# Decoder of a four-layer convolution kernel: last step by eight rows, with parts of the next group's front between its halves

## The chip, the cores and the metric

The kernel runs on one core of a Trainium2 chip. The metric is the device time of one execution in microseconds (us). The core has a matrix engine (PE, with its weight loads shown as PEld), a vector engine (DVE), a scalar engine (ACT), a general engine (POOL), and SP, which here only issues transfers (DMAs). Each engine works through its own queue in order, and waits on semaphores where it needs what another engine or a DMA makes. SBUF is the on-chip memory of 128 partitions, PSUM the small memory that PE writes to.

## The reference

Four layers are applied to x, 16 images of 32 channels of 128x128, in float32; each adds its result to its input. The change lies in layer 3, an edge detector followed by a small encoder and decoder. The 16 images of 32 channels are taken as 4 groups of 4 x 32 channels of 128x128.

```python
# layer 3: y = edge operators of x, five of them, concatenated
y = maxpool2(conv3x3(y, conv1_w, conv1_b))      # 128 -> 64
y = maxpool2(conv3x3(y, conv2_w, conv2_b))      # 64 -> 32
y = maxpool2(conv3x3(y, conv3_w, conv3_b))      # 32 -> 16
y = conv3x3(y, conv4_w, conv4_b)                # 16
y = conv3x3(deconv2x2(y, deconv1_w, deconv1_b), conv5_w, conv5_b)   # -> 32
y = conv3x3(deconv2x2(y, deconv2_w, deconv2_b), conv6_w, conv6_b)   # -> 64
y = conv3x3(deconv2x2(y, deconv3_w, deconv3_b), conv7_w, conv7_b)   # -> 128
return x + orig * y                             # orig: x normalised
```

## The kernel before

`network` (line 2137) runs the stages one after another: `layer0`, three stages of layer 1, `layer2`, then `layer3_edges` (line 1436: edge operators, conv1 and its pooling along one axis; result in the DRAM scratch `p1`), and last `layer3_net` (line 1892), everything from conv2 on. This last stage is called the decoder stage here. Its parts:

- **Joint weights** (lines 1903 to 1955). Each deconvolution and the convolution after it are one linear map, so their weights are multiplied once: for k = 5, 6, 7 three loads (`d_t`, `d_b`, `c_t`, each in one buffer), 36 matmuls of 32x32 and nine of one column (each is two passes on PE), a copy to `W`, and eight small DVE operations for a bias and an edge correction (lines 1930 to 1952).
- **front(g)** for one group of four images (all 128 partitions: 4 images x 32 channels). It loads `p1` in eight tiles `pt` of 512 KB (two buffers), takes a maximum on DVE (line 2078) and writes `c2` with two ACT operations each (line 2080). `squares` (line 1980) then gathers shifted copies of `c2` with 16 SBUF-to-SBUF DMAs of 136 KB, so that one matmul sees four pixels x 32 channels as its 128 rows. `conv_pool` (matmuls line 1998) does conv2 and the pooling, 8 PSUM tiles of 16 matmuls; then 16 DMAs of 36 KB, conv3, conv4 (line 354), `windows` (line 2033; 16 DMAs of 36 KB), joint step 5, 16 DMAs of 136 KB, joint step 6 (lines 2046 to 2070). The result is `d3`, one buffer.
- **The last step** of a group: `windows(d3)` makes `w7` with 16 DMAs of 528 KB, all before the first matmul. Then for each q of 8 parts of 16 output rows: load `xs` (1024 KB), normalise it to `xn` on ACT (line 2119), four phases of four matmuls (line 2046), an edge correction per phase (line 2051), a multiply into `xn` (line 2126), the addition of `xs` on DVE (line 2127), and the store of `xn` from ACT's queue (line 2128). `xs` and `xn` have two buffers each.

Each matmul of the decoder has 32 columns of weights and writes 32 partitions; the four images j = 0..3 go to four column tiles of PE, which can work at the same time.

**Order.** Within the decoder stage nothing fixes the order of the engines' queues by hand: the tile framework orders the instructions of each queue by readiness and by their place in the program. Other stages use `in_order` (line 48), which makes the named engines follow the program's order; `layer3_edges` does not. The loop of the stage, before, is

```python
        d3 = front(groups[0])
        for n, g in enumerate(groups):
            w7 = windows(d3, 64, "w7")
            if n + 1 < len(groups):
                d3 = front(groups[n + 1])
            for q in range(8):
                ...
```

so the next group's front stands ahead of this group's eight parts.

**The edge stage's beginning** (lines 1451 to 1527) makes constants in a pool `et`, which is closed before the pools of the strips are opened; the first work on strips is at line 1587, and PE's first work after the constants waits for statistics of two images (line 1648).

Of the kernel before, what the change touches and what calls it, by code (L numbers as in the profile page):

```python
# [10 lines left out]
F32 = mybir.dt.float32  # L11
# [1424 lines left out]
def layer3_edges(tc, w, x3, p1, sb3, b3, groups=range(NG)):  # L1436
# [12 lines left out]
    with ExitStack() as ctx:  # L1449
# [20 lines left out]
        with tc.tile_pool(name="et", bufs=1) as tp:  # L1470
# [56 lines left out]
            V.tensor_scalar_mul(V5[:, 14], V5[:, 14], -1.0)  # L1527
        ap = ctx.enter_context(tc.tile_pool(name="ea", bufs=2))
# [345 lines left out]
        for m, b in enumerate(images):  # L1874
            now = nxt
            more = m + 1 < len(images)
            if more:
                g1, j1 = divmod(images[m + 1], 4)
                t1 = image(g1, j1)
            for n in range(4):  # L1880
                conv(n, now, d)
                if m < 3 or made < 12 * (m + 2) + 4 * n:
                    advance(min(made + 4, 12 * len(images) + 1))
                if n == 2 and more:
                    if m + 1 in cut_at:
                        vec = batch(m + 1)
                    nxt = prepare(g1, j1, t1, *expand(j1), vec)
            if more:
                d = differences(t1)


def layer3_net(tc, w, x3, p1, out, sb3, b3, groups=range(NG)):
# [4 lines left out]
    nc = tc.nc  # L1897
    with ExitStack() as ctx:
        cp = ctx.enter_context(tc.tile_pool(name="fc", bufs=1))
        psum = ctx.enter_context(tc.tile_pool(name="fp", bufs=7, space=PSUM))  # L1900
        psw = ctx.enter_context(tc.tile_pool(name="fpw", bufs=1, space=PSUM))
        wc = {i: load(nc, cp, w[f"c{i}_p"], f"c{i}_p") for i in range(2, 4)}
        wc4 = load(nc, cp, w["c4_w"], "c4_w")
        bb = load(nc, cp, w["l3_b"], "l3_b")

        pairs = {
            (0, 0): [(0, 1)], (0, 1): [(1, 0), (2, 1)],
            (1, 0): [(0, 0), (1, 1)], (1, 1): [(2, 0)],
        }
        joint = {}  # L1910
        with tc.tile_pool(name="fw", bufs=1) as tp:
            for i, k in ((1, 5), (2, 6), (3, 7)):
                wd = load(nc, tp, w[f"d{i}_t"], "d_t")
                bd = load(nc, tp, w[f"d{i}_b"], "d_b")
                wk = load(nc, tp, w[f"c{k}_t"], "c_t")
                pw = psw.tile([P, 4, T], F32, name="pw", tag="pw")
                for s in range(4):
                    first = True
                    for ph in range(4):
                        rows, cls = pairs[ph // 2, s // 2], pairs[ph % 2, s % 2]  # L1920
                        todo = [(dy, dx, p, q) for dy, p in rows for dx, q in cls]
                        for n, (dy, dx, p, q) in enumerate(todo):
                            nc.tensor.matmul(
                                pw[32 * s : 32 * s + 32, ph], wd[:, 2 * p + q],
                                wk[:, 3 * dy + dx, 0:T], start=first, stop=n == len(todo) - 1,
                                tile_position=(0, 32 * s), skip_group_check=True,
                            )
                            first = False
                W = cp.tile([P, 4, T], F32, name=f"W{k}", tag=f"W{k}")
                nc.vector.tensor_copy(W, pw)  # L1930


                pb = psw.tile([P, 4, T], F32, name="pb", tag="pw")
                for t in range(9):
                    nc.tensor.matmul(
                        pb[:, 0, t : t + 1], wk[:, t], bd, start=(t == 0), stop=(t == 8),
                        skip_group_check=True,
                    )
                tb = tp.tile([P, 3, 3], F32, name="tb", tag="tb")
                nc.vector.tensor_copy(tb.rearrange("p a b -> p (a b)"), pb[:, 0, 0:9])  # L1940
                by = tp.tile([P, 2, 3], F32, name="by", tag="by")
                nc.vector.reduce_sum(by[:, 0], tb, AX.X)
                nc.vector.reduce_sum(by[:, 1], tb.rearrange("p a b -> p b a"), AX.X)
                bias = cp.tile([P, 1], F32, name=f"B{k}", tag=f"B{k}")
                nc.vector.reduce_sum(bias, by[:, 0], AX.X)
                nc.vector.tensor_add(bias, bias, bb[:, k - 2 : k - 1])
                edge = cp.tile([P, 8], F32, name=f"E{k}", tag=f"E{k}")
                nc.vector.tensor_scalar_mul(
                    edge[:, 0:4].rearrange("p (a b) -> p a b", b=2), by[:, :, 0:3:2], -1.0
                )  # L1950
                for a in range(2):
                    nc.vector.tensor_copy(
                        edge[:, 4 + 2 * a : 6 + 2 * a], tb[:, 2 * a, 0:3:2]
                    )
                joint[k] = W, bias, edge

# [29 lines left out]
        def conv_pool(i, src, n, put):  # L1986
# [4 lines left out]
            for r in range(0, h, nr):  # L1991
                m = sp.tile([P, nr, h], F32, name="m", tag="m")
                for ph in range(4):
# [11 lines left out]
                    if ph == 0:  # L2005
                        nc.scalar.activation(m, ps, AF.Identity, bias=b)
                    else:
                        nc.vector.scalar_tensor_tensor(m, ps, b, m, ALU.add, ALU.max)
                put(r, m)

# [5 lines left out]
        def pitched(n, tag):  # L2016


            t = bp.tile([P, n + 3, n + 1], F32, name=tag, tag=tag)
# [20 lines left out]
        def phase(k, src, n, ph, i0, nr):  # L2040
# [10 lines left out]
            nc.vector.tensor_scalar_add(ps[:, :, c], ps[:, :, c], edge[:, 2 + b : 3 + b])  # L2051
            if (a == 0 and i0 == 0) or (a == 1 and i0 + nr == n):
                r = a * (nr - 1)
                nc.vector.tensor_scalar_add(ps[:, r], ps[:, r], edge[:, a : a + 1])  # L2054
                o = ps[:, r, c : c + 1]
                nc.vector.tensor_add(o, o, edge[:, 4 + 2 * a + b : 5 + 2 * a + b])  # L2056
            return ps, bias

        def joint_conv(k, src, n, dst):
            nr = min(n, 512 // n)  # L2060
            for i0 in range(0, n, nr):
                for ph in range(4):
# [4 lines left out]
                    if b:  # L2067
                        nc.vector.tensor_scalar_add(o, ps, bias)  # L2068
                    else:
                        nc.scalar.activation(o, ps, AF.Identity, bias=bias)  # L2070

        def front(g):
            c2 = planes(ap, 64, "c2")
            for h in range(4):
                for a in range(2):
                    t = xp.tile([P, 2, 8, 64], F32, name="pt", tag="pt")
                    nc.sync.dma_start(t, p1[g][:, 2 * a : 2 * a + 2, 8 * h : 8 * h + 8])
                    nc.vector.tensor_tensor(t[:, 0], t[:, 0], t[:, 1], ALU.max)
                    for b in range(2):
                        nc.scalar.activation(  # L2080
                            c2[:, a, b, a + 8 * h : a + 8 * h + 8, b : b + 32], t[:, 0, :, b:64:2],
                            AF.Identity, bias=b3[:, g : g + 1],
                        )
            c3 = planes(bp, 32, "c3")

            def put(r, m):
                r //= 2
                nr = m.shape[1] // 2
                for a in range(2):
                    for b in range(2):  # L2090
                        nc.scalar.copy(
                            c3[:, a, b, a + r : a + r + nr, b : b + 16], m[:, a::2, b::2]
                        )

            conv_pool(2, squares(c2, 64, "w6"), 64, put)
            c4 = padded(bp, 16, "c4")
            conv_pool(
                3, squares(c3, 32, "w5"), 32, lambda r, m: nc.scalar.copy(c4[:, 1:17, 1:17], m)
            )
# [3 lines left out]
            nc.scalar.activation(d1[:, 1:17, 1:17], ps, AF.Identity, bias=bb[:, 2:3])  # L2103
            d2 = pitched(32, "d2")
            joint_conv(5, windows(d1, 16, "w5"), 16, d2)
            d3 = pitched(64, "d3")
            joint_conv(6, windows(d2, 32, "w6"), 32, d3)
            return d3

        d3 = front(groups[0])  # L2110
        for n, g in enumerate(groups):
            w7 = windows(d3, 64, "w7")
            if n + 1 < len(groups):
                d3 = front(groups[n + 1])
            for q in range(8):
                xs = xp.tile([P, 2048], F32, name="xs", tag="xs")
                nc.sync.dma_start(xs, x3[g][:, 2048 * q : 2048 * q + 2048])
                xn = xp.tile([P, 2048], F32, name="xn", tag="xn")
                nc.scalar.activation(  # L2119
                    xn, xs, AF.Identity, bias=sb3[:, g, 1:2], scale=sb3[:, g, 0:1]  # L2120
                )
                xv = xn.rearrange("p (i a j b) -> p a b i j", a=2, j=64, b=2)
                for ph in range(4):
                    ps, bias = phase(7, w7, 64, ph, 8 * q, 8)
                    v = xv[:, ph // 2, ph % 2]
                    nc.vector.scalar_tensor_tensor(v, ps, bias, v, ALU.add, ALU.mult)  # L2126
                nc.vector.tensor_add(xn, xn, xs)  # L2127
                nc.scalar.dma_start(
                    out[4 * g : 4 * g + 4].rearrange("b c h w -> (b c) (h w)")[
                        :, 2048 * q : 2048 * q + 2048  # L2130
                    ],
                    xn,
                )
# [252 lines left out]
```

## Time and profile before

| what | us |
|---|---|
| median of three runs | 17326.91 (17290.49 to 17357.52) |
| the profiled execution | 17413.58 |
| its span, first to last instruction | 17411.8 |
| decoder stage in it, from the end of the edge stage's matmuls at 16577 | 835 |
| DVE, POOL and PE busy over the whole span | 14898.3, 9787.4, 15201.4 |
| mean granted PE clock over the span | 0.92 |

All times below are of the profiled execution, in us from the start of its span, so the stage begins at 16577 and ends at 17412. In a view by windows, each row is a stretch of time: its length, busy time (and instruction count) of PE, PEld, DVE, ACT and POOL in it, the granted PE clock, the mean busy share of the 16 DMA engines, and GB/s. In a timeline, a row is a run of equal instructions: start, length, engine, line, operation, output <- input, count, and in brackets the idle time before it with what ended it. "SPq" is SP issuing a DMA. Every matmul of float32 counts as two PE instructions.

### The profile page before, as it was taken

How to read it: one execution, taken by the hardware profiler on the slowest of the kernel's cores; microseconds unless marked ns; L12 is line 12 of the kernel's file. 1: busy time of each engine (PE TensorE's matmuls, PEld its weight loads, DVE VectorE, ACT ScalarE, POOL GpSimd, SP SyncE). 2: the span in 40 equal slices, each digit the busy share in tenths (PEclk: the TensorE clock that was granted, in tenths of full speed). 3: DMA queues.
4: the chain of work that ended last, by engine and by line, in shares of the span. 5: the costliest groups of instructions: out<-in, count | busy, mean ns of one | idle time of the engine just before them, and what ended most of it. 6: DMA issues, size and time to landing. Idle time of an engine off the chain costs nothing. (4 is left out here: it accounts for less than half of the span.)

```text
span 17411.8 us, 300873 instructions
## 1 busy us (share of the span) xinstructions
PE 15201.4 (87%) x113294; PEld 5760.5 (33%) x113294; DVE 14898.3 (86%) x15100; ACT 12226.0 (70%) x23748; POOL 9787.4 (56%) x18465
## 2 busy tenths in 40 slices
PE   8999999999998889888888888899999997688965
PEld 2333333333333322222222222255555553233422
DVE  9999999999999758999899999888888886787623
ACT  7878887878887656777677776588888883465411
POOL 8999999999999617778787787700000000000000
PEclk9999999999999988999899999889999898787888
DMA  0000000000000384444454444477777779544346
GB/s 19 14 12 12 12 12 16 12 12 12 12 12 12 61 149 152 162 160 160 157 166 157 156 161 159 141 198 193 196 204 193 194 194 200 115 82 77 66 134 197
DMA packets 1532120, 1895.18 MB, mean 109 GB/s; under 512 B 150885, under 2 KB 872861, under 8 KB 1519846
## 3 DMA queue, kind: packets, MB, share of 16 engines
q1 hardware_dynamic: 1419558, 1698.68, 37.7%
q10 hardware_dynamic: 84480, 83.91, 1.5%
q0 software_dynamic: 26624, 93.35, 1.5%
q8 instruction: 891, 14.60, 0.3%
q14 instruction: 567, 4.64, 0.1%
HBM read 1560.92 MB, written 229.64 MB: 103 GB/s over the span
## 5 line engine op out<-in xcount | busy, mean ns | idle before, releaser
L235 POOL TENSOR_SCALAR Rp<-su,nv 128x128 f32<-128x128 f32 x16384 | 5807.8, 395 | 142.2 <-PE pS L241 108.5
L224 DVE TENSOR_TENSOR Rd<-pu,nv 128x2048 f32<-128x2048 f32 x2176 | 4878.2, 2277 | 64.3 <-PE pS L241 61.2
L239 ACT ACTIVATE Ra<-su,bv 128x128 f32<-128x128 f32 x14336 | 4284.4, 388 | 601.0 <-PE pS L241 594.3
L241 PE MATMUL pS<-Rd,zw 128*32 128x512 f32 x17408 | 2883.8, 604 | 315.9 <-DVE Rd L224 314.7
L822 DVE TENSOR_TENSOR_SCAN hh<-dd,state,pd 128x512 f32<-128x512 f32 x2304 | 2824.0, 1267 | 165.2 <-PE py L856 23.5
L843 POOL TENSOR_TENSOR hh<-hh,bc 128x2048 f32<-128x2048 f32 x512 | 2318.7, 4529 | 501.3 <-DVE state L830 472.6
L241 PE MATMUL pS<-Rp,zw 128*32 128x512 f32 x8192 | 1937.0, 596 | 145.3 <-POOL Rp L235 140.7
L807 PE MATMUL pd<-du,spread 32*128 32x512 f32 x4608 | 1386.5, 677 | 549.2 <-DVE hh L822 541.0
L1228 POOL DMA_DIRECT2D x<-ob x64 | 90.0, 1407 | 3098.5 <-DVE ob L1227 2762.7
L799 ACT ACTIVATE dd<-dd,m_a 128x512 f32<-128x512 f32 x2304 | 1513.8, 714 | 336.7 <-DMA dd<-dm 324.9
L817 DVE TENSOR_TENSOR pd<-pd,bc 128x1024 f32<-128x1024 f32 x1152 | 1401.4, 1216 | 66.9 <-ACT bc L780 50.6
L1236 ACT ACTIVATE yd<-yd,nrow 128x2048 f32<-128x2048 f32 x512 | 1242.2, 2426 | 41.3 <-DMA yd<-ymap 41.3
L241 PE MATMUL pS<-Ra,zw 128*32 128x512 f32 x7168 | 1256.3, 602 | 0.0
L1116 ACT ACTIVATE ya<-pb,nrow 128x1024 f32<-128x1024 f32 x1024 | 1185.9, 1247 | 83.9 <-PE pb L1115 83.4
L1115 PE MATMUL pb<-Y,sel 32*128 32x512 f32 (+1 forms) x5120 | 1083.5, 741 | 163.4 <-ACT ya L1116 160.2
L241 PEld LDWEIGHTS pS<-Rd,zw 128*32 128x32 f32 x17408 | 603.3, 109 | 1368.1 <-DVE Rd L224 734.0
L807 PEld LDWEIGHTS pd<-du,spread 32*128 32x128 f32 x4608 | 381.6, 195 | 1617.9 <-DVE hh L822 701.1
L1120 DVE TENSOR_SCALAR yd<-yd 128x2048 f32<-128x2048 f32 x512 | 719.9, 1406 | 190.4 <-ACT yd L1236 188.8
L241 PEld LDWEIGHTS pS<-Rp,zw 128*32 128x32 f32 x8192 | 432.4, 110 | 1236.9 <-POOL Rp L235 773.9
L1120 DVE TENSOR_SCALAR ya<-ya 128x2048 f32<-128x2048 f32 x512 | 755.1, 1475 | 9.5 <-ACT ya L1116 8.3
L1127 PE MATMUL pd<-ya,xt 128*32 128x128 f32 x16384 | 688.8, 311 | 45.8 <-DVE ds L1280 34.5
L1127 PEld LDWEIGHTS pd<-yd,xt 128*32 128x32 f32 x16384 | 539.1, 178 | 465.4 <-issue 218.0
(423 smaller groups left out, 23535.7 us busy)
## 6 DMA issues: line engine op xcount, KB each, us to landing
dd<-dm SPq DMA_DIRECT2D x2304, 256.0 KB
yd<-ymap SPq DMA_DIRECT2D x512, 1024.0 KB
hw<-x SPq DMA_DIRECT2D x192, 512.0 KB
dm<-dt POOLq DMA_DIRECT2D x192, 256.0 KB, 3.5
xb<-tok SPq DMA_DIRECT2D x248, 144.0 KB
w<-d SPq DMA_DIRECT2D x64, 528.1 KB
x<-in_x SPq DMA_DIRECT2D x64, 512.0 KB
x<-o SPq DMA_DIRECT2D x128, 256.0 KB
```

The source lines that it names most:

```text
L224: nc.vector.tensor_tensor(R, st["pu"].unsqueeze(1).to_broadcast([P, 4, 4, HW]), nv[:, :, i::32].rearrange("p t q -> p q t").unsqueeze(3).t ...
L235: nc.gpsimd.tensor_scalar(R[:, q, k], su[:, k], 3.4028234e38, nv[:, k, c], ALU.min, ALU.max)
L239: nc.scalar.activation(R[:, q, k], su[:, k], AF.Relu, bias=bv[:, k, c])
L241: nc.tensor.matmul(st["pS"][32 * q : 32 * q + 32], zw[:, 31 - i : 63 - i], R[:, q], start=first, stop=False, tile_position=(0, 32 * q), sk ...
L799: S.activation(dd[:, r], dd[:, r], AF.Exp, scale=acol[:, dr, d : d + 1])
L807: nc.tensor.matmul(pd[:, a], spread[e, k], st["du"][n][e], start=True, stop=True)
L817: V.tensor_mul(pd, pd, bm.unsqueeze(1).to_broadcast([P, 2, CH]))
L822: V.tensor_tensor_scan(hh[:, r, s], dd[:, r, s], pd[:, a, s], st["state"][:, 4 * i + r : 4 * i + r + 1], ALU.mult, ALU.add,)
L843: G.tensor_mul(hh, hh, st["bc"][1, n].unsqueeze(1).to_broadcast([P, 4, CH]))
L1120: V.tensor_scalar(t, t, 1.0, 1.0, ALU.min, ALU.subtract)
L1127: M(pd[32 * q : 32 * q + 32, i], xt[:, :, xc], h, start=True, stop=True, tile_position=(0, 32 * q),)
L1236: S.activation(yd, yd, AF.Abs, bias=nrow)
```

## The change

It has four parts.

1. The joint weights move into a function `joint_weights`, called at the end of the edge stage's constants inside the pool `et`; their results live in the pool `keep`.
2. The last step fetches its windows part by part: `fetch(g, d, q)` issues, for nine rows of `d3`, 16 DMAs of 32 partitions x 2340 bytes (73 KB each) and the load of `xs`, two parts ahead; `w7`, `xs` and `xn` have three buffers, `d3` two, `pt` four. The four phases become two halves (b = 0, 1) in PSUM tiles of two banks (two buffers); the other convolutions have four PSUM banks in place of seven.
3. `front` becomes a generator with 17 places to pause. In each part q, `last` runs one piece of the next group's front after the matmuls of each half, and the loop runs a third piece after it.
4. PE, DVE and ACT follow the program's order in the whole stage (`in_order`). The final addition moves from DVE to POOL, and the store from ACT's queue to POOL's.

```diff
-def layer3_edges(tc, w, x3, p1, sb3, b3, groups=range(NG)):
+def layer3_edges(tc, w, x3, p1, sb3, b3, keep, groups=range(NG)):
...
             V.tensor_scalar_mul(V5[:, 14], V5[:, 14], -1.0)
+            joint = joint_weights(nc, w, keep, tp, psg, "pg")
         ap = ctx.enter_context(tc.tile_pool(name="ea", bufs=2))
...
-        psum = ctx.enter_context(tc.tile_pool(name="fp", bufs=7, space=PSUM))
-        psw = ctx.enter_context(tc.tile_pool(name="fpw", bufs=1, space=PSUM))
+        psum = ctx.enter_context(tc.tile_pool(name="fp", bufs=4, space=PSUM))
+        psl = ctx.enter_context(tc.tile_pool(name="fpl", bufs=2, space=PSUM))
...
+                    if ph == 1:
+                        yield
                 put(r, m)
+                yield
...
+        def front(g, res):
+
             c2 = planes(ap, 64, "c2")
+            ts = []
+
+            def rows(n):
+                h, a = divmod(n, 2)
+                t = xp.tile([P, 2, 8, 64], F32, name="pt", tag="pt", bufs=4)
+                nc.sync.dma_start(t, p1[g][:, 2 * a : 2 * a + 2, 8 * h : 8 * h + 8])
+                ts.append(t)
+
+            for n in range(4):
+                rows(n)
+            yield
+            for n in range(8):
+                t = ts[n]
...
+                if n < 4:
+                    rows(n + 4)
+                if n == 3:
+                    yield
+            src = squares(c2, 64, "w6")
+            yield
+            yield
...
+        def fetch(g, d, q):
+
+            wq = sp.tile([P, 4, 9, 65], F32, name="w7", tag="w7", bufs=3)
+            flat = d.rearrange("p r c -> p (r c)")
+            for j in range(4):
+                for s in range(4):
+                    o = 65 * (8 * q + s // 2) + s % 2
+                    nc.sync.dma_start(
+                        wq[32 * s : 32 * s + 32, j].rearrange("p r c -> p (r c)"),
+                        flat[32 * j : 32 * j + 32, o : o + 9 * 65],
+                    )
+            xs = xp.tile([P, 2048], F32, name="xs", tag="xs", bufs=3)
+            nc.sync.dma_start(xs, x3[g][:, 2048 * q : 2048 * q + 2048])
+            return wq, xs
+
+        def last(g, q, now, beside):
...
+            for b in range(2):
+                ps = psl.tile([P, 2, 8, 64], F32, name="pl", tag="pl")
...
+                next(beside, None)
+                o = ps[:, :, :, 63 * b]
+                V.tensor_scalar_add(o, o, edge[:, 2 + b : 3 + b])
...
+                for a in range(2):
+                    v = xv[:, b, a]
+                    V.scalar_tensor_tensor(v, ps[:, a], bias, v, ALU.add, ALU.mult)
+            G.tensor_add(xn, xn, xs)
+            G.dma_start(
...
+        with in_order(tc, nc.tensor, V, S):
+            for _ in front(groups[0], res):
+                pass
+            steps = [(g, q) for g in groups for q in range(8)]
+            ahead = [fetch(*(lambda g, q: (g, res[g], q))(*steps[n])) for n in range(2)]
+            beside = iter(())
+            for n, (g, q) in enumerate(steps):
+                if q == 0:
+                    m = groups.index(g) + 1
+                    beside = front(groups[m], res) if m < len(groups) else iter(())
+                now = ahead.pop(0)
+                last(g, q, now, beside)
+                next(beside, None)
+                if n + 2 < len(steps):
+                    g2, q2 = steps[n + 2]
+                    if g2 != g:
+                        for _ in beside:
+                            pass
+                    ahead.append(fetch(g2, res[g2], q2))
```

## The prediction

> **What bounds the kernel now.** The page gives a span of 17411.8 us inside an execution of 17413.58; the change touches only the last stage and 39 us that it moves. So I read the view by windows over that stage first, cut where the timelines show a front or a last step to end.
>
> ```profile
> core 0: us, PE busy (x) PEld busy (x) DVE busy (x) ACT busy (x) POOL busy (x), PEclk, DMA share, GB/s
> 16577.00:16616.00 39.00, 22.34 (x270) 21.77 (x270) 4.68 (x30) 4.66 (x4) 0.40 (x4) 0.53 0.38 128
> 16616.00:16747.00 131.00, 88.86 (x498) 30.77 (x498) 24.91 (x59) 22.52 (x51) 2.07 (x20) 0.82 0.39 110
> 16747.00:16793.00 46.00, 0.00 (x0) 0.00 (x0) 0.04 (x1) 0.00 (x0) 0.45 (x3) 0.53 0.97 200
> 16793.00:16901.00 108.00, 88.79 (x527) 31.18 (x528) 18.88 (x53) 16.18 (x35) 1.80 (x18) 0.88 0.32 87
> 16901.00:16961.00 60.00, 38.85 (x280) 11.26 (x279) 44.63 (x79) 14.96 (x12) 0.57 (x4) 0.83 0.80 262
> ...
> 17242.00:17299.00 57.00, 30.87 (x228) 8.55 (x220) 43.15 (x77) 12.57 (x6) 0.00 (x0) 0.79 0.72 247
> 17299.00:17342.00 43.00, 24.20 (x44) 5.41 (x45) 2.29 (x2) 0.00 (x0) 0.00 (x0) 0.78 0.96 240
> 17342.00:17412.00 70.00, 34.00 (x213) 8.90 (x211) 46.15 (x80) 16.75 (x8) 0.00 (x0) 0.77 0.60 226
> ```
>
> Row by row: joint weights; first front; the 16 large window DMAs with every engine still; second front (group 1); last step of group 0. Front and last step then alternate, 108+60, 110+62 and 109+57: a period of about 169 us a group. The final two rows are the last group: its windows, then its eight parts. No engine is full: DVE works 19 of 108 and 45 of 60 us. The DMA engines are full only while large windows move (0.97). The stage is a chain of waits, and SP's and PE's timelines for group 1's front say which:
>
> ```profile
> 16835.48 10.01 SPq L1980 DMA_DIRECT2D w<-c  x16
> 16859.90 25.12 SPq L2033 DMA_DIRECT2D w<-d  x32
> ```
>
> ```profile
> 16793.32 40.96 PE L1998 MATMUL ps<-w,c_p 128*32 128x512 f32 x256 [47.95 <-DMA w<-c]
> ...
> 16855.13 4.12 PE L354 MATMUL ps<-c,c_w 128*128 128x256 f32 x18 [1.16 <-ACT c L2098]
> 16863.71 1.89 PE L2046 MATMUL ps<-w,W 128*32 128x256 f32 x4 [4.45 <-DMA w<-d]
> ...
> 16879.51 32.80 PE L2046 MATMUL ps<-w,W 128*32 128x512 f32 x184 [6.32 <-DMA w<-d]
> ```
>
> Sixteen DMAs of 36 KB take SP 10.0 us, 0.63 each; the second SP row holds two such sets. Conv2 takes 41 us although PE has 28.2 to 29.5 us of work (later groups' rows, 256 instructions without a gap). conv3's squares start at 16835.5 and conv4 begins at 16855.1: 19.6. Conv4 to d1: 4.8. From there to joint step 5's end 15.0, and joint step 6 ends at 16901, 26 later. In the last step the list of waits names the two-buffer loop of `xn`:
>
> ```profile
> ACT xn L2119 <- DMA out<-xn: 161.1, 22, 16.2
> ```
>
> **The change, part by part.**
>
> *Joint weights leave the stage.* The first front starts when the edge stage's memory is free, at about 16580. Eight `pt` at SP's pace in the old first front (six in 13.13 us: 2.19 each) are 17.5, with 3.9 for the first landing (issued 16583.67, used 16587.59) and 1.6 for the last maximum and its ACT pair: c2 at 16603, where it was 16635. Sixteen squares 10 to 12.4, 2 landing, conv2 28.4 (8 x 3.55): 43, where the old one took 46 to 49. The remaining 66 us (16681 to 16747) lose 4, since program order runs the four column tiles together in joint step 6, where its PE row stretches over arriving windows. So d3 stands at about 16709 instead of 16747.
>
> *Their new place.* PE is idle there for 101.64 us (first fence below), so 270 PE instructions cost it nothing. One chain took 10.6 and 11.0 us per k (starts of the `c_t` loads). Nine small DVE operations x 3 are 4.2 us. DVE is busy until 15001.5 and then waits 11.36 us for strips (second fence):
>
> ```profile
> 15082.92 0.59 PE L1648 MATMUL pm<-ms,avg 128*128 128x5 f32 x2 [101.64 <-DVE ms L1644]
> ```
>
> ```profile
> 15013.01 2.58 DVE L1587 TENSOR_TENSOR R<-a 128x2322 f32<-128x2322 f32 x1 [11.36 <-DMA a<-x]
> ```
>
> If the first copy waits for DVE's queue (15001.5), the chain ends near 15030; the strips' buffers reuse the memory of the constants' pool, so line 1587 would start 17 later. Ends: 0 (copies slip in early, or other memory) and 22 (all three links after 15001.5). This stretch is DVE's, then PE's, so it passes to the end. I take 17.
>
> *Fetch by parts.* The 46 us of large windows become the first fetch: 17 issues and a landing, 13. The first part starts at 16722. But each part now issues 17 DMAs, 10.4 us of SP, for 1.2 MB; a group has 128 + 64 short ones (0.63), 8 `xs` (0.33) and 8 `pt` (0.37): 126 us of SP. The DMA engines had 110 x 0.65 + 62 x 0.83 = 123 us of work in the period from 16961; 9.6 MB in place of 8.7 adds 5 at 200 GB/s: 128. Here a rule speaks against the change: the Trainium skill (DMA: Bandwidth & Descriptors, Rules for kernel authors and Anatomy of one DMA) says to join transfers, since below 64 KB one pays mostly overhead, 2.0 us fixed each. Taken one after another that is 16 x 2.2 = 35 us a part, 280 a group. The SP rows decide otherwise: 36 KB DMAs follow each other at 0.63, and joint step 5 used the last at 16871.9, 2 us after its issue. Overhead overlaps; SP's issue stays.
>
> *Pieces beside parts.* A group's front has 17 pauses and three pieces run per part, so it ends within parts 0 to 5; PE, DVE and ACT queue in program order, so the second half's matmuls of a part, its DVE work and the next part's `xn` stand behind whatever piece waits for a DMA; SP's fetches stand behind squares or before them. So the front's own chain still sets the parts' pace:
> - part 0: four `pt` more, behind one or two fetches in the DMA queue (1.2 MB at 205 GB/s + 1 MB at 350 = 9 us each, halves of it hidden) plus 8.8 of their own and 2 of landing, maxima and ACT: 25
> - squares: 12
> - conv2 28.4, three halves of a last step between its pieces (1.8 each), the copies: 36
> - squares, conv3: 19.6 and part of a half: 22
> - conv4: 5; windows, joint step 5: 15; windows 10 + 2, joint step 6 8, two halves 4: 24
> - d3 to next part 0: a fetch after the one under way: 17
> - short sets that find SP within a fetch (half of 10.4, three of four): 15
>
> Sum 171, against 169. What the last step gains by standing beside the front is given back to SP's issue and to the waits that now stand in one order. The gain left is at the two ends: the first d3 is 38 earlier, and behind the last d3 stand 17 + 101 us where 57 + 43 + 70 stood.
>
> *The last group.* Per part the DMA engines need 1.2 MB at 205 to 218 GB/s and 2.1 at 350: 11.5, over SP's 10.4 and DVE's 4. Eight parts with the last one's tail (`xn` 2.1, halves 5, POOL 4.5 and 1.4, store 8): 101.
>
> *Addition and store on POOL.* Nearest row:
>
> ```profile
> L843 POOL TENSOR_TENSOR hh<-hh,bc 128x2048 f32<-128x2048 f32 x512 | 2318.7, 4529 | 501.3 <-DVE state L830 472.6
> ```
>
> Same shape: 4.5 us in place of 2.28 on DVE; a store's issue on POOL takes 1.4 (row L1228) against 0.34. With three buffers 2.1 + 5 + 4.5 + 1.4 + 9.6 (L1228's median landing) = 23 us stay under three parts; cost 2 us at the very end, counted above. The skill's SBUF — State Buffer (SBUF: two separate sides) says that a DVE operation with two SBUF inputs and a GpSimd operation exclude each other for a whole instruction. Here only the `pt` maxima qualify (line 2126 reads PSUM): by the rule up to two per group wait 4.5, 27 us in all. No row shows such a wait; line 843's 512 additions, beside DVE's scans, lie within 4502 to 4567 ns. I take 0 and keep 27.
>
> *PSUM, clock.* Four banks instead of seven hold 14 us of conv2, whose evacuation takes 0.75: nothing. The granted clock is 0.82 to 0.88 in the fronts' rows; if pieces with gaps drop it, conv2 at 0.75 costs 9 a group more: kept as a bound.
>
> Sum: 16722 + 3 x 171 + 101 = 17336, + 17 = 17353, against 17412: -59, 0.3% of the profiled execution. The runs' median is 17327 and the stage's share of it the same: 17268.
>
> **Rivals.**
> *Overlap works.* If loads run ahead (SP orders `pt` and fetches by readiness, so part 0's 25 and the 17 and 15 shrink), a period comes near its bound, 128 plus a landing or two: 140. Then -59 - 93 = -152: 17175. For it: SP hoisted `pt` and `xs` far ahead before. Against: only four `pt` buffers, and the first fetch of a group needs all of d3.
> *SP's order turns against it.* If each of the four short sets stands behind a fetch that itself waits for its `w7` buffer, which PE frees only behind the piece that needs that set's forerunner, each costs 10.4 and about 10 of waiting: +65 a group over the 15 counted, period 236, 17464. Break-even with before is a period of 191, a loss over 0.5% starts at 220. For it: SP's list shows `xs` waiting up to 23 us at its head. Against: fetches are two parts ahead.
> *It doesn't shorten anything*: edge stage 22 later, `pt` behind POOL 27, clock 27: 17327, the time before.
>
> **How the numbers follow.** Forecast 0.64 (17268, own range 17215 to 17330: period 157 to 182, edge 0 to 22, part of POOL's 27), overlap 0.22, SP against it 0.06, nothing gained 0.08. The range 17170 to 17350 leaves out about half of the overlap's lower side and SP's case. A measurement of this kernel tells 0.5% (87 us) from no change: faster takes the overlap and 0.11 of the forecast's shortest periods, 0.33; slower 0.06; same 0.61.
>
> **What would show it.** Part 0 to part 0 (line of `xn`) 171 apart, with parts 0 to 3 of 20 to 35 us and 6 and 7 short; first d3 near 16709 (plus the shift); line 1587 later by 0 to 22 and PE's wait for `ms` near 119; SP issuing in most of a period; POOL's addition at 4.5. A period under 150 or over 191, or an edge stage that ends more than 25 off, proves me wrong.

## The result and the profile after

| | before | after |
|---|---|---|
| median of 20 runs each, us | 17342.08 (17290.49 to 17397.22) | 17309.66 (17282.1 to 17345.11) |
| ratio, 95% interval | | 0.9981 [0.9973, 0.9989], -19 to -47 us |
| span of the profiled execution | 17411.8 | 17302.5 |
| layer 2's last matmul | 14955.1 | 14855.2 |
| edge stage (from there to its own last large matmul) | 1618.4 | 1662.7 |
| decoder stage (from there to the end) | 838.3 | 784.6 |
| the two changed stages together | 2456.7 | 2447.3 |

The spans differ by 109 us, but 100 of these lie ahead of any changed instruction: in the kernels measured here, all with the same code up to that point, the last scan (a long DVE loop ahead of layer 2) begins anywhere from 11127.5 to 11279.2. So I compare the two changed stages, each from its own start. There the profile shows -9.4 us where -59 was forecast. The decoder stage gained 54, not 76, and the edge stage lost 44, not 17. (Timed, the gain is 32. Over the fourteen kernels measured against before, the difference in the two stages of one profile and the timed difference agree within 23 us, so 9 and 32 are not told apart.)

**Decoder stage after**, view by windows: first front; two periods, part 0 to part 0 of the next group; the last group.

```profile
core 0: us, PE busy (x) PEld busy (x) DVE busy (x) ACT busy (x) POOL busy (x), PEclk, DMA share, GB/s
16521.00:16649.00 128.00, 70.86 (x498) 23.24 (x498) 21.37 (x52) 16.29 (x36) 2.86 (x32) 0.72 0.44 131
...
16831.00:17015.00 184.00, 116.04 (x764) 34.37 (x756) 52.59 (x109) 32.33 (x43) 43.29 (x37) 0.79 0.66 198
17015.00:17196.50 181.50, 113.55 (x754) 33.77 (x754) 51.54 (x107) 32.30 (x43) 41.08 (x16) 0.78 0.67 200
17196.50:17302.50 106.00, 54.68 (x224) 11.08 (x224) 26.83 (x53) 16.74 (x8) 40.62 (x16) 0.79 0.72 235
```

The still rows of before are gone, yet a period is 182.5 us (before 169 for a front and a last step one after the other), with no engine and not the DMA engines (0.67) full. The one queue that works nearly throughout is SP's. Its timeline over the same period:

```profile
16831.26 7.06 SPq L2149 DMA_DIRECT2D w<-d  x9
16838.43 0.51 SPq L2154 DMA_DIRECT2D xs<-x  x1
16838.99 11.99 SPq L2092 DMA_DIRECT2D pt<-p  x8
16851.02 1.15 SPq L2149 DMA_DIRECT2D w<-d  x2
16859.11 10.22 SPq L1988 DMA_DIRECT2D w<-c  x16
...
16935.29 11.90 SPq L2044 DMA_DIRECT2D w<-d  x16
16947.23 7.55 SPq L2149 DMA_DIRECT2D w<-d  x12
16954.88 0.53 SPq L2154 DMA_DIRECT2D xs<-x  x1
16955.52 13.32 SPq L2044 DMA_DIRECT2D w<-d  x16
16968.89 10.15 SPq L2149 DMA_DIRECT2D w<-d  x16
16979.14 1.62 SPq L2154 DMA_DIRECT2D xs<-x  x1
16980.85 10.68 SPq L2149 DMA_DIRECT2D w<-d  x16
16991.63 1.47 SPq L2154 DMA_DIRECT2D xs<-x  x1
16993.27 15.65 SPq L2149 DMA_DIRECT2D w<-d  x16
17009.02 0.54 SPq L2154 DMA_DIRECT2D xs<-x  x1
```

Added up, SP's rows cover 158 of the 184 us (8 of them are waits between the loads of `pt` for a free buffer); three waits, for `c2`, `c3` and `d1` (7, 10 and 7 us), make nearly all of the rest. Line 2149, the windows by parts, takes 93 us for 128 DMAs. ACT, whose `xn` opens each part, shows who waits for that:

```profile
16982.23 0.77 ACT L2081 ACTIVATE d<-ps,B 128x512 f32<-128x512 f32 x1 [1.49 <-PE ps L2057]
16986.05 2.10 ACT L2161 ACTIVATE xn<-xs,sb 128x2048 f32<-128x2048 f32 x1 [3.05 <-DMA xs<-x]
17002.61 2.09 ACT L2161 ACTIVATE xn<-xs,sb 128x2048 f32<-128x2048 f32 x1 [14.46 <-DMA xs<-x]
17015.09 2.09 ACT L2161 ACTIVATE xn<-xs,sb 128x2048 f32<-128x2048 f32 x1 [10.39 <-DMA xs<-x]
```

ACT's last piece of `d3` ends at 16983.0. SP has just begun the fetch of part 7 of the running group (16980.85) and issues that of the next group's part 0 only behind it (16993.27). Part 0 begins 32 us after `d3`: 10 for the rest of part 7's fetch, 16 for its own windows, 6 for the issue and landing of `xs`.

**Edge stage after.** PE's waits for the statistics `ms` after, then the same views of before (its first wait was shown above):

```profile
14997.06 0.56 PE L1649 MATMUL pm<-ms,avg 128*128 128x5 f32 x2 [80.06 <-DVE ms L1645]
...
15061.58 0.59 PE L1649 MATMUL pm<-ms,avg 128*128 128x5 f32 x2 [10.76 <-DVE ms L1645]
15063.12 0.56 PE L1655 MATMUL pv<-ms,avg 128*128 128x5 f32 x2 [0.95 <-DVE ms L1653]
...
15273.85 0.60 PE L1649 MATMUL pm<-ms,avg 128*128 128x10 f32 x2 [52.56 <-DVE ms L1645]
```

```profile
15146.87 0.59 PE L1648 MATMUL pm<-ms,avg 128*128 128x5 f32 x2 [7.33 <-DVE ms L1644]
...
15192.97 0.28 PE L1654 MATMUL pv<-ms,avg 128*128 128x5 f32 x2
...
15326.43 0.60 PE L1648 MATMUL pm<-ms,avg 128*128 128x10 f32 x2 [28.49 <-DVE ms L1644]
```

From layer 2's end, the first wait ends at 141.9 (before 127.8): 14 late, as forecast. But the third ends at 418.7 (before 371.3): 47 late. In between the order is another: `pv` (a variance) follows the second wait's mean `pm` at once, where before it came 46 us later.

### The profile page after: what moved, and what is told of

Its sections match the earlier page's. It is cut to its first block, busy times and chain, and to the rows that moved or that the text cites. A ratio compares the mean times of both kernels' runs of the same rounds, so it can differ in the third digit from the quotient of the medians.

```text
span 17302.5 us, 301334 instructions
## 1 busy us (share of the span) xinstructions
PE 15122.8 (87%) x113294; PEld 5719.3 (33%) x113294; DVE 14784.8 (85%) x15004; ACT 12224.8 (71%) x23748; POOL 9973.4 (58%) x18529
## 5 line engine op out<-in xcount | busy, mean ns | idle before, releaser
L241 PE MATMUL pS<-Rp,zw 128*32 128x512 f32 x8192 | 2006.3, 596 | 172.0 <-POOL Rp L235 169.8
```

Of the source, the lines that this page charges most:

```text
L241: nc.tensor.matmul(st["pS"][32 * q : 32 * q + 32], zw[:, 31 - i : 63 - i], R[:, q], start=first, stop=False, tile_position=(0, 32 * q), sk ...
```

## The experiments

The questions were two: where do the edge stage's 44 us come from, and what sets the period of 182. Theory for the edge stage: the constants' pool, whose memory the strips reuse (rival: PE, DVE and SP being busy with the joint weights). Theory for the decoder (C in the quoted texts): SP's issue of many small windows (rivals: the DMA engines, the two-part look-ahead, few `pt` buffers, POOL's addition). No experiment changes the look-ahead alone. All kernels from e3 on keep e3's edit, so that the edge stage doesn't disturb.

| kernel | edge stage | decoder | period, mean of three | last group | ratio, 95% interval |
|---|---|---|---|---|---|
| after | 1662.7 | 784.6 | 182.5 | 106.0 | 0.9981 [0.9973, 0.9989] |
| e1 | 1623.6 | 811.6 | 183.0 | 104.7 | 0.9978 [0.997, 0.9986] |
| e2 | 1662.1 | 809.7 | | | 1.001 [0.9998, 1.0021] |
| e3 | 1627.9 | 787.0 | 182.8 | 106.3 | 0.9966 [0.9955, 0.9977] |
| e4 | 1617.6 | 795.6 | 182.2 | 106.9 | 0.997 [0.996, 0.998] |
| e5 | 1624.3 | 714.6 | 163.8 | 87.6 | 0.9937 [0.9923, 0.995] |
| e6 | 1624.2 | 1059.8 | 249.7 | 176.6 | 1.0133 [1.0118, 1.0147] |
| e7 | 1628.0 | 780.9 | 181.2 | 106.1 | 0.9971 [0.9961, 0.998] |
| e8 | 1628.6 | 787.8 | 180.5 | 112.0 | 0.9974 [0.9966, 0.9982] |
| e9 | 1628.6 | 899.6 | | | 1.0042 [1.0029, 1.0056] |
| e11 | 1628.3 | 813.5 | 178.7 | 138.5 | 0.9978 [0.997, 0.9987] |
| e12 | 1624.1 | 773.1 | 170.8 | 121.5 | 0.9967 [0.9958, 0.9977] |
| e13 | 1623.7 | 804.5 | 183.4 | 116.7 | 0.9969 [0.9957, 0.9981] |
| e14 | 1624.4 | 759.1 | 178.7 | 85.5 | 0.9948 [0.9936, 0.996] |

### e1 and e2: the joint weights alone

e1 takes part 1 of the change back and keeps the rest; e2 is the kernel before with part 1 only.

```diff
# e1
-            joint = joint_weights(nc, w, keep, tp, psg, "pg")      # layer3_edges
+        with tc.tile_pool(name="fw", bufs=1) as tp, tc.tile_pool(name="fpw", bufs=1, space=PSUM) as psw:
+            joint, bb = joint_weights(nc, w, cp, tp, psw, "pw")    # layer3_net
```

> Stages are measured in the profile: the edge stage from the last matmul of layer 2 to its own last 512-column matmul (1618 us before, 1663 after), the decoder stage from there to the end (838 before, 785 after). Theory A (the 44 us that the edge stage lost come from the joint weights' new place): edge stage back at 1618, decoder about 785 + 36 = 821, together 17 us under before: ratio 0.9990. Rival B (the edge stage differs from run to run, the place of the joint weights is not the cause): edge stage anywhere from 1618 to 1663, ratio at that of the change plus 36 us: 1.0002.

> Before, with nothing changed but the joint weights' place. Theory A: edge stage about 1663, decoder about 838 - 36 = 802, together 9 us over before: ratio 1.0005. Rival B: edge stage 1618, decoder 802: ratio 0.9979.

The edge stage stands at 1623.6 without the move and at 1662.1 with it alone, so the 39 to 44 us belong to it and to nothing else in the change. The decoder gets 27 us (e1: 811.6 against 784.6) to 29 (e2: 809.7 against 838.3). Moving the weights is thus a loss of some 12 to 15 us as it was done: they were cheap where they stood. e2's ratio doesn't contradict it (1.001, no change within its interval). Its PE shows the same wait of 52.56 us for `ms`.

### e3 and e4: the memory of the constants' pool

e3 gives the joint weights' loads a pool that lives as long as the stage. e4 also makes them at the stage's end.

```diff
# e3
+        jp = ctx.enter_context(tc.tile_pool(name="ej", bufs=1))
-            joint = joint_weights(nc, w, keep, tp, psg, "pg")
+            joint = joint_weights(nc, w, keep, jp, psg, "pg")
# e4: as e3, but called last in layer3_edges
-        return joint
+        return joint_weights(nc, w, keep, jp, psg, "pg")
```

> After, with the joint weights' loads and small tiles in a pool of their own, so that no strip waits for their memory. Theory A1 (14 us of the 44 are that wait): the first operation on strips (R<-a) 58 us behind layer 2's last matmul in place of 72, edge stage 1648, ratio 0.9973. Theory A2 (the 14 us are the DVE work itself or SP's loads in front of the strips'): R<-a stays at about 72, edge 1663, ratio 0.9981.

> As with the own pool, and the joint weights come last in the edge stage's program, so that every other instruction of the stage stands ahead of them by program order. Theory A (the other 30 us come from an order of the edge stage that the joint weights' place disturbs): edge stage about 1618 to 1625, ratio 0.9957. Rival: the order changes whenever any work is added, edge stage at about 1648 again, ratio 0.9973.

In the kernel after, SP loads `d_t`, `d_b`, `c_t` three times, each time when the one buffer is free, and the strips' loads (line 1551) stand behind the last:

```profile
14884.66 0.34 SPq L34 DMA_DIRECT2D d_t<-in_d_t  x1
14888.59 0.32 SPq L34 DMA_DIRECT2D d_b<-in_d_b  x1
14888.96 0.41 SPq L34 DMA_DIRECT2D c_t<-in_c_t  x1
...
14902.79 0.32 SPq L34 DMA_DIRECT2D d_t<-in_d_t  x1
14906.71 0.32 SPq L34 DMA_DIRECT2D d_b<-in_d_b  x1
14907.08 0.41 SPq L34 DMA_DIRECT2D c_t<-in_c_t  x1
...
14917.82 1.94 SPq L1551 DMA_DIRECT2D a<-x  x4
```

The last `c_t` is issued at 14907.5 and read until 14917.0 by PE; 0.8 later SP loads `a`, and DVE's first copy `R` follows at 14927.45, 72.2 after layer 2's end (before 57.9). With its own pool (e3) the copy comes at 63.0, the loads of `a` follow 0.6 us after the start of the last `c_t`, and the long wait for `ms` behind is that of before:

```profile
15281.24 0.60 PE L1650 MATMUL pm<-ms,avg 128*128 128x10 f32 x2 [28.49 <-DVE ms L1646]
```

That gives back 35 of the 44 us, though the copy comes only 9 earlier: the larger part is not the delay but the other order of the two images' work, which goes with the shared memory: in e2, as after, that `pv` follows its `pm` at once (15081.15, 15082.69), in e3, as before, 45 us later (15101.42, 15146.57). What in the framework's ordering tips it is not shown. e4 gives back all 44, and pays 9 of them in the decoder, whose first part comes 142 us after the stage's start (after: 131). Both stages together stand 32 (e3) and 34 us (e4) below the kernel after. The rival is refuted by e3: the same work on the same engines, with other memory. With its own pool the move is worth 20 us in the two stages (e1 2435.2, e3 2414.9).

### e5 and e6: fewer and more window transfers

e5 fetches 17 rows for two parts at a time (64 DMAs of 138 KB a group, with 6% fewer bytes, where there were 128); e6 halves each window, so that the same bytes take 256.

```diff
# e5
+            if q % 2 == 0:
+                wq = sp.tile([P, 4, 17, 65], F32, name="w7", tag="w7", bufs=2)
...
-                        flat[32 * j : 32 * j + 32, o : o + 9 * 65],
+                            flat[32 * j : 32 * j + 32, o : o + 17 * 65],
# e6
+                    for lo, hi in ((0, 5), (5, 9)):
...
+                            flat[32 * j : 32 * j + 32, o + 65 * lo : o + 65 * hi],
```

> The version with its own pool (e3: parts' period 183 us a group, last group 106, ratio 0.9966), with windows fetched for two parts at once: the same 16 DMAs for 17 rows, so half as many short DMAs per group. Theory C (SP's issue of short DMAs, about 0.75 us each here, and what queues behind it sets the period): 64 fewer x 0.75 = 48 us less on SP, period 150 to 160, last group about 95, ratio about 0.991. Rival D (the front's own chain of landings and program-order waits sets the period, SP only fills it): period 175 to 183, ratio 0.996.

> e3 with every window DMA cut into two (five rows and four), the same bytes in twice as many issues. Theory C: 33 issues a part, some 21 us of SP, period near 255, last group near 180, ratio about 1.013. Rival D: period under 195 and last group about 110, ratio 0.998; if the DMA engines' bytes were the bound, nothing changes.

e6 came as theory C had it (250, 177 and 1.0133 for 255, 180 and 1.013): a period is 67 us longer for 128 more issues. Its last group, SP's timeline and windows:

```profile
17438.54 0.53 SPq L2156 DMA_DIRECT2D xs<-x  x1
17439.16 21.89 SPq L2151 DMA_DIRECT2D w<-d  x32
```

```profile
17351.00:17527.70 176.70, 73.12 (x230) 12.95 (x225) 26.87 (x54) 16.75 (x8) 40.45 (x16) 0.64 0.42 136
```

One transfer follows the other at 0.68 us with the DMA engines 0.42 busy: issue, not bytes, is the price. e5 makes a period 19 us shorter and the last group 19, and is the best version: 17162.67 against 17296.45. Its period, 163.8, lies between C's 150 to 160 and D's 175 to 183, so the price of issue is not all there. e5 also holds the windows of up to four parts, where three were held, so that a part of its gain may be a longer look-ahead; e6 leaves the look-ahead as it was. What is next in e5 is told by its windows, the third period and part of the last group:

```profile
16885.70:17045.50 159.80, 103.37 (x753) 35.27 (x754) 51.98 (x107) 32.33 (x44) 41.12 (x16) 0.79 0.74 218
...
17053.00:17118.00 65.00, 40.42 (x196) 9.22 (x192) 19.57 (x37) 12.57 (x6) 29.70 (x13) 0.74 0.92 288
```

In that part of the last group the DMA engines are 0.92 busy at 288 GB/s; over the period SP's rows cover 114 us of 160 and the DMA engines are 0.74 busy, so neither is full.

### e7 and e8: buffers of `pt`, addition on DVE

```diff
# e7
-                t = xp.tile([P, 2, 8, 64], F32, name="pt", tag="pt", bufs=4)
+                t = xp.tile([P, 2, 8, 64], F32, name="pt", tag="pt", bufs=8)
# e8
-            G.tensor_add(xn, xn, xs)
+            V.tensor_add(xn, xn, xs)
```

> e3 with eight buffers for pt instead of four, so all of a group's p1 tiles can be loaded ahead. Theory C says the pt loads sit in SP's queue and the DMA queue in front of part 0's squares: part 0 falls from 28 us to about 15, period 170, ratio 0.9945. Rival: the loads are then issued no earlier, since SP is busy with fetches; period 183, ratio 0.9966.

> e3 with the last addition back on DVE (the store stays on POOL). In the changed kernel some maxima of pt, which take 0.69 us, took up to 4.9 beside POOL's addition, about 9 us in three groups. If that is the mutual exclusion of two-input DVE work and POOL, every maximum is 0.69 here. Time: 9 us won, 2.3 a part given back where DVE is waited for in program order, at most 7 parts x 2.3 x 3 = 48: ratio between 0.9961 and 0.9990.

Neither moves the time (intervals overlap with e3's). What e8 tells is what the addition on POOL does to the maxima of `pt` on DVE, which read SBUF twice. The groups, before the experiment (kernel after) and in e8:

```profile
L2183 POOL TENSOR_TENSOR xn<-xn,xs 128x2048 f32<-128x2048 f32 x32 | 145.1, 4536 | 388.5 <-DVE xn L2182 290.5 <-issue 72.8 <-DVE pl L2174 25.1
...
L2101 DVE TENSOR_TENSOR pt<-pt 128x512 f32<-128x512 f32 x32 | 31.0, 991 | 43.8 <-DMA pt<-p 43.7
```

```profile
L2102 DVE TENSOR_TENSOR pt<-pt 128x512 f32<-128x512 f32 x32 | 21.6, 690 | 50.0 <-DMA pt<-p 49.9
```

In the kernel after, three maxima, each while POOL adds, take 2989 to 4898 ns, and the mean is 991; in e8 all take 681 to 693. That is 9 us over four groups, and e8, without them, is no faster.

### e9: the front not beside the parts

```diff
-                    beside = front(groups[m], res) if m < len(groups) else iter(())
+                    for _ in front(groups[m], res) if m < len(groups) else ():
+                        pass
```

> e3 (period 183, last group 106, ratio 0.9966) with the whole of the next group's front in front of part 0, in place of pieces beside the parts; everything else, fetches by part too, stays. If pieces beside parts hide anything, the period is the front alone, about 110, and eight parts at SP's 13 = 104, less the first fetches: about 205, and the ratio 3 x 22 us higher, 1.0004. If the front's waits are SP's anyway (theory C in its strict form), 183 and 0.9966.

The decoder is 113 us longer than in e3, so the pieces beside the parts are worth 113, where some 66 were expected, and the change without them is a loss (1.0042). In a stretch with nothing but parts SP's rows are:

```profile
16981.86 11.97 SPq L2150 DMA_DIRECT2D w<-d  x16
16993.94 1.46 SPq L2155 DMA_DIRECT2D xs<-x  x1
```

A part is 13.3 us there (starts of `xn`), and SP's fetch is all of it.

### e11 to e14: is it `xs` in the same queue?

SP's fetch took 12.5 us, 0.78 a window, where 0.63 was counted. Theory E: windows wait behind the 1 MB of `xs` in the same DMA queue. Theory F: it is the windows' own price. e11 and e13 issue the load of `xs` from ACT and from POOL; e12 and e14 the same in e5.

```diff
# e11, e12 (with e5's fetch)
-            nc.sync.dma_start(xs, x3[g][:, 2048 * q : 2048 * q + 2048])
+            nc.scalar.dma_start(xs, x3[g][:, 2048 * q : 2048 * q + 2048])
# e13, e14 (with e5's fetch)
+            G.dma_start(xs, x3[g][:, 2048 * q : 2048 * q + 2048])
```

> e3 with xs loaded from ACT's queue, two parts ahead as before. In the changed kernel a fetch takes SP 12.9 us in the last group where 17 issues at the old pace would be 10.4. Theory E: the 2.5 us are SP standing behind the 1 MB of xs in its own DMA queue; then a fetch takes 10.1 here, the last group 8 x 10.6 + 10 = 95 (or 11.5 a part by the DMA engines: 102), the period 183 - 18 = 165, ratio 0.993. Rival F: a 73 KB window DMA costs SP 0.77 by itself; period 178 (only the issue of xs leaves SP, 0.6 a part), last group 102, ratio 0.996.

> Fetches of 16 rows (e5: period 164, last group 88, ratio 0.9937) and xs from ACT's queue together. Theory E: SP loses another 8 x 2.5 us a group, period about 150, last group 88 (DMA engines busy 0.92 there already), ratio 0.991. Rival F: period 160 to 164, ratio 0.9935.

> As e3_joint_own_pool, but the load of xs is issued by POOL, whose queue holds nothing but the additions and the stores, so no engine with work of the parts waits behind it (in e11 ACT did). Theory E, SP's window transfers stall because they queue behind the 1 MB of xs in the same DMA queue: a fetch takes SP 10 us or less where it took 12.4, eight of them 20 us less in a group, period about 162 where it was 183, last group about 90, ratio 0.9925. Theory F, a window transfer costs SP what it costs by itself (its own descriptors and the load on the DMA engines), whatever else stands in the queue: SP is rid only of the issue of xs, 0.5 us a part, period 178 or more, last group 102 or more, ratio 0.995 to 0.997.

> As e5_fetch_16_rows, with the load of xs issued by POOL. SP has half the window transfers here and no longer sets the pace of the last group, where the DMA engines are 0.92 busy. By theory E the period falls from 164 towards 155 and the ratio to 0.992; by theory F it stays within 4 us of 164, last group about 87, ratio 0.993 to 0.994. Should ACT wait for xs no longer (it waited because xs is issued behind the windows of its part), a few us a group are gained in either theory.

The times give no clean answer. In e11 and e12 the load waits on ACT for the buffer that POOL's addition frees, and the parts' `xn` stand behind it (list of waits of e11):

```profile
ACT xn L2162 <- POOL xn L2184: 84.4, 7, 21.2
```

In e13 the period is 183.4 and the last group 116.7, far from E's 162 and 90. In e14 the period is 178.7, where e5 has 163.8 and neither theory had more than 168. Other work of POOL, the clearing of padding (line 2032 in e13) that waits for DMAs, now stands ahead of loads.

SP's issues taken one by one decide it: neither theory holds. The shortest, the median and the longest issue, for the windows by parts after, for the squares after (half of them 36 KB, half 136 KB), and for part of e13, where no `xs` is in SP's queue:

```profile
L2149 SPq DMA_DIRECT2D w<-d x512: 507/589/2337, 16646.0 to 17280.7; - x171
L1988 SPq DMA_DIRECT2D w<-c x128: 507/589/1514, 16542.4 to 17101.3; - x128
L2150 SPq DMA_DIRECT2D w<-d x134: 507/589/1657, 16899.7 to 17089.5; - x134
```

The median is 589 ns for all, and some 44 ns lie between two issues: that is the 0.63 counted, for 73 KB as for 36. In the timeline of the period above, the fetch at 16968.89 takes 10.15 us, 0.63 a window. So F falls. What raises the mean to 0.78 is a few long issues. Here is one fetch of the last group, cut at the long ones, with POOL's row beside it:

```profile
17230.00 3.07 SPq L2149 DMA_DIRECT2D w<-d  x5
17231.86 0.58 POOL L2184 DMA_DIRECT2D out<-xn  x1 [0.30 <-POOL xn L2183]
17233.12 3.64 SPq L2149 DMA_DIRECT2D w<-d  x2
17236.81 5.80 SPq L2149 DMA_DIRECT2D w<-d  x9
```

The first five windows, right behind the issue of `xs` (17229.37), follow each other at 0.62: so E falls too. The two long ones come behind POOL's issue of the store. Over the whole stage after, 134 of SP's 768 issues of windows and squares start within 5 us of a store's issue. In them lie 45 of the 57 us by which the long issues (over 0.65 us) exceed 0.589. That is about 1.5 us a store. Behind the 1 MB loads that have no issue of POOL within 6 us, the excess is 0.1 us when SP issued them (e3, nine loads) and 0.3 when ACT did (e11, eight). The fetch of part 0 that took 15.65 us meets two stores:

```profile
16990.29 0.57 POOL L2184 DMA_DIRECT2D out<-xn  x1 [0.30 <-POOL xn L2183]
...
16996.10 0.58 POOL L2184 DMA_DIRECT2D out<-xn  x1 [0.30 <-POOL xn L2183]
```

So the change's own move of the store goes with the slower fetch. Whether POOL's queue or the store's bytes hold SP up stays open: every kernel here with windows by parts stores from POOL, and none was run with the store on another queue.

## Why the prediction was right and wrong

The prediction had the sign right and the size wrong: its sum of -59 stands against -9 in the profile's two stages and -32 timed. Some 27 us of the difference are in the edge stage, 35 in the three periods and 5 in the last group; the first part came 14 earlier than forecast. One of the signs that it had named as proving it wrong came: the edge stage ends more than 25 us off (44 where 17 was forecast). Term by term:

| step | predicted | measured |
|---|---|---|
| edge stage's end | +17 (0 to 22) | +44 |
| edge stage's end to the first `d3` (its first fetch) | 132 | 128 |
| edge stage's end to the first part 0 (line of `xn`, whose `xs` was loaded ahead) | 145 | 131 |
| period | 171 | 182.5 |
| part 0 to the first squares | 25 | 27.8 |
| squares and conv2 | 12 + 36 | 45.2 |
| conv3 with its squares; conv4 | 22; 5 | 26.3; 4.7 |
| windows and joint step 5; joint step 6 | 15; 24 | 20.2; 27.5 |
| `d3` to the next part 0 | 17 | 32.1 |
| short sets behind a fetch | 15 | in the rows above |
| last group | 101 | 106.0 |

("Edge stage's end" is here the start of its last large matmul; the prediction counted from 16577, 3.5 us after that start in the kernel before. The inner rows are from the period that begins at 16831.35; they sum to 183.8.)

- **Edge stage: the step that failed is its upper end of 22.** The mechanism (memory reused by the strips, copies late) was right and gave 14 us against 17. Not foreseen was another order of the two images' work, for 30 more. The prediction priced the shared memory as a shift alone, though nothing fixes the order of that stage. e3 showed it: 9 us less delay, 35 us back.
- **Period: the step that failed is "d3 to next part 0: a fetch after the one under way: 17".** The step is right in kind, and its size was wrong: 32. The fetch under way had 10 us to go and not half of its 10.4; the first fetch took 15.7 and not 10.4, with two stores in it; `xs` took 6 to be issued and land. The other terms with "short sets" come to 152 against 154, but not each by itself: conv3 to `d3` took 79 where 66 stood, and the lump of 15 for short sets made up for it.
- **SP's sum.** 126 us a group were counted; SP's rows cover 158. The price of 0.63 was right, though the prediction read it off with a slip: of the "two such sets" in its second SP row, one is of 36 KB (`d1`) and one of 136 KB (`d2`). Of the 32 us more, 14 are long issues, 9 the row of `pt` (12 for the 3 counted, mostly waits for its four buffers) and 4 `xs`. **The term put too low is "Addition and store on POOL".** It priced POOL's own time (2 us at the very end) and nothing for SP, whose issues are held up by about 1.5 us behind each store, some 12 us a group. This also makes the last group: 13.0 a part on SP, 1.9 of them long issues, where the DMA engines' 11.5 was to be the bound.
- **The rule against the change.** The Trainium skill (DMA: Bandwidth & Descriptors, Rules for kernel authors) says to join transfers. The prediction set aside its own estimate from that page (35 us a part), rightly: a fetch took 12.5. (The 2.0 us stand there, in Anatomy of one DMA, for DMAs that GpSimd issues; these are SP's.) But it didn't ask what the advice would still be worth at SP's own row: e5, which joins transfers that are above the page's 64 KB already, gains 70 us in the decoder.
- **Right:** DVE's exclusion by POOL (Trainium skill, SBUF — State Buffer, SBUF: two separate sides) showed, 9 us of the bound of 27, and cost no time, as taken; POOL's addition took 4.5 (4536 ns); the gain at the two ends is there. The store's issue took POOL 0.57, less than the 1.4 allowed. The lower clock of 0.79 in the periods' rows had been kept as a bound of 9 us a group; squares and conv2 took 45.2 us where 48 stood.
- **Rivals.** "Overlap works" (140) did not come: four `pt` of the second group were loaded far ahead, but those of the third stand in SP's full queue until part 0 has begun (16838.99). "SP's order turns against it" has the right engine, but with 182.5 it stays short of its own break-even of 191.
- **Open:** timed, the gain is 32 and in the profile's two stages 9; one profile a kernel can't part these.

## What to carry to other kernels

When a large transfer is cut up to overlap with other work, price the queue that issues it: the number of DMAs times the pace of a row of the same kind, added up over the period against the time that the change wants to reach. Look at what stands in that queue when the critical result appears, and at what other engines issue beside it. A mean that is higher than expected should be split into single issues before a theory is built on it. Moving work into an idle stretch of an engine is free only if its buffers don't share memory with what comes next; give it a pool of its own. Where no order is written, shared memory can cost several times the delay that it causes.

## What was not expected of the hardware

- SP's issue of a DMA from SBUF to SBUF (32 partitions) took 0.59 us in the median for 36 and 136 KB (squares after), 37 KB (e6), 73 KB (after) and 138 KB (e5): its size made no difference.
- Behind POOL's issue of a 1 MB store, SP's own issues took about 1.5 us longer in sum (after), for a reason that is not shown.
- POOL issued a store in 0.57 us in the decoder, where line 1228's took 1.43.
- A DVE maximum of 0.69 us stretched to 4.9 us beside an addition on POOL, while POOL's own addition took 4.53 to 4.83 us there and 4.54 in the mean.
